# When a strip's norm is issued, and which engine adds its squares, in the fusions of the last two images

## The chip, the core and the metric

The kernel runs on one core of a Trainium2 chip. TensorE multiplies matrices, VectorE (DVE in the profile), ScalarE (ACT) and GpSimd (POOL) work elementwise, SyncE (SP) issues most transfers. The metric is the device time of one execution in microseconds (us); the median of several runs is compared.

## What is computed

The input is four images of 512 channels and 64 x 64 pixels, all in float32. Layer 0 is a linear attention with depthwise convolutions, a projection and the residual. Layer 1, cut to what matters here (`x` is layer 0's result):

```
E = stack([sobel, lap, diag, grad])                    # edge maps of x
ef = gelu(batch norm of (w_branch @ E))                # 4 branches, 512 channels
att = sigmoid(w_att2 @ gelu(w_att1 @ mean(ef) + b1) + b2)
z = w_fuse @ (ef * att) + b_fuse
zn = (z - mean_c(z)) / sqrt(var_c(z) + 1e-6)           # over the 512 channels
out = gelu(zn * ln_gamma + ln_beta) + x
```

The last three lines are the fusion. The kernel takes the mean out by centring the weights and the bias, so that the variance of a pixel is the sum of the squares of its 512 values of `z`, divided by 512.

## The kernel before

Four stages follow each other for an image: its attention (TensorE's convolutions and projections), `project_out` (products `yps`, writing layer 0's result `y` to memory), `edge_branches` (VectorE and ScalarE make `maps` from a window of `y`, TensorE multiplies them by the branch weights, products `br`, ScalarE's Gelu writes `ef` to memory), and `fuse_out`. Each stage is a Python generator that yields after a piece of work; the main loop runs one image's attention and lets the image before it advance behind it, by costs written out (`SHARE_F`, `FILL_F` and others, in estimated us). TensorE's order is exactly the order in which the program issues its products. On the other engines and on SP the framework orders the instructions by its own estimate, within what the data allow; each engine then works through its queue strictly in order.

At the end no attention is left. The last image's `project_out` and `edge_branches` (in taller steps of 8 rows, `side == "left"`) are interleaved with the third image's fusion through `fill` (L1001): after each edge step, as many yields of the fusion are taken as `FILL_F` and `FILL_EACH` say. Then the last image's fusion runs alone. I number images 0 to 3.

The fusion of an image (L794) goes over 8 strips of 512 pixels (`pieces`; the last strip of image 3 is cut into two halves of 256). For a strip it loads four chunks `ef`, and for each of four chunks `c` of output channels calls `fuse(c)` (L845):

- L848: four products into a PSUM bank `zps`, with the weights `wf_sb`
- L850: ScalarE squares it, with the bias, into `total` (c = 0) or `sq`
- L853 or L855: the value itself is drained, with the bias, to a buffer `z`, by ScalarE for image 2 and by VectorE for the others; there are 6 such buffers
- L858: for c > 0 GpSimd adds `sq` to `total`

`norm` (L860) finishes a strip: L864 multiplies `total` by a matrix of ones, so that each partition holds the sum over all channels (product `var`, in a PSUM bank); L866 is ScalarE's square root, L867 VectorE's reciprocal. Then for each chunk: SP loads `yr`, a part of `y` (L872, two buffers), VectorE multiplies `z` by the reciprocal (L875), ScalarE applies the Gelu (L876), GpSimd adds `yr` (L879), and SP stores `z` to `out` (L880). Only when that store has landed is the buffer of `z` free. The norm of a strip is held back and issued within the next strip's four calls: after the second of them (L900). `zps`, `var` and the small products of the attention weights share four PSUM banks in rotation (`ps_tile`); the tall edge step uses four others.

So TensorE's order in a strip is `zps` 0, `zps` 1, `var` of the strip before, `zps` 2, `zps` 3. A product can start only when the bank that was used four products of this kind earlier has been read.

Of the kernel before, what the change touches and what calls it, by code (L numbers as in the profile page):

```python
# [8 lines left out]
F32 = mybir.dt.float32  # L9
# [4 lines left out]
B, C, H, W = 4, 512, 64, 64  # L14
N = H * W
P = 128
NCH = C // P
# [72 lines left out]
def conv_seq_kernel(  # L90
    ctx: ExitStack, tc, x, wqkv, dpk, wtab, proj, projc, pwk, bn0, consts, vec, watt1, batt1, watt2, wbr, wfuse, out
):
    nc = tc.nc
# [18 lines left out]
    def ps_tile(name):  # L112
        return psum.tile([P, 512], F32, tag="ps", name=name)
# [8 lines left out]
    def rows(ap, width=W):  # L122
        return ap.rearrange("p (r c) -> p r c", c=width)
# [79 lines left out]
    def center_bias():  # L203

        fb_ps = ps_tile("fb_ps")
        nc.tensor.matmul(fb_ps[:, 0:4], lhsT=ones, rhs=vec_sb[:, V_FB, :], start=True, stop=True)
        fb_mean = const.tile([P, 1], F32, name="fb_mean")
        nc.vector.tensor_reduce(fb_mean, fb_ps[:, 0:4], AX.X, ALU.add)
        nc.vector.tensor_scalar(fb_mean, fb_mean, 1.0 / C, None, ALU.mult)
        nc.vector.tensor_scalar(fbias, vec_sb[:, V_FB, :], fb_mean, None, ALU.subtract)  # L210
# [583 lines left out]
    def fuse_out(b, efs, pool_sb, side):  # L794

        y = ys[b % 2]
        with ExitStack() as stack:
            pool = stack.enter_context(tc.tile_pool(name=f"F{b}", bufs=2, side=side, reuse_waits="tile"))
            wf_sb = pool.tile([P, NCH, C], F32, name="wf_sb", bufs=1)
            nc.sync.dma_start(out=wf_sb, in_=wfuse)  # L800
            watt1_sb = pool.tile([P, NCH, 64], F32, name="watt1_sb", tag="sq", bufs=3)
            nc.sync.dma_start(out=watt1_sb, in_=watt1)
            watt2_sb = pool.tile([64, C], F32, name="watt2_sb", tag="sq", bufs=3)
            nc.sync.dma_start(out=watt2_sb, in_=watt2)
            wf_mean = small.tile([P, NCH], F32, name="wf_mean")
            nc.vector.tensor_reduce(wf_mean, wf_sb, AX.X, ALU.add)
            nc.vector.tensor_scalar(wf_mean, wf_mean, 1.0 / C, None, ALU.mult)
            yield 0.0


            pooled = small.tile([P, 4], F32, name="pooled")
            nc.vector.tensor_reduce(pooled, pool_sb, AX.X, ALU.add)
            yield 14.0
            if b == 0:
                center_bias()
            hid_ps = ps_tile("hid_ps")
            for k in range(4):
                nc.tensor.matmul(
                    hid_ps[0:64, 0:1], lhsT=watt1_sb[:, k, :], rhs=pooled[:, k : k + 1], start=(k == 0), stop=(k == 3)
                )  # L820
            hid = small.tile([64, 1], F32, name="hid")
            nc.scalar.activation(hid, hid_ps[0:64, 0:1], AF.Gelu, bias=batt1_sb, scale=1.0 / N)
            yield 4.0
            att_ps = ps_tile("att_ps")
            for k in range(4):
                nc.tensor.matmul(att_ps[:, k : k + 1], lhsT=watt2_sb[:, ts(k, P)], rhs=hid, start=True, stop=True)
            att = small.tile([P, 4], F32, name="att")
            nc.vector.tensor_add(att, att_ps[:, 0:4], vec_sb[:, V_ATT2, :])
            nc.scalar.activation(att, att, AF.Sigmoid)

            for k in range(4):
                nc.vector.tensor_scalar(
                    wf_sb[:, k, :], wf_sb[:, k, :], wf_mean[:, k : k + 1], att[:, k : k + 1], ALU.subtract, ALU.mult
                )
            yield 8.0


            share = SHARE_F / (NJ * 5)


            pieces = [(j, 0, 512) for j in range(NJ)]
            if b == B - 1:
                pieces[-1:] = [(NJ - 1, 0, 256), (NJ - 1, 256, 512)]

            def fuse(c, ef, zs, total, n):  # L845
                ps = ps_tile("zps")[:, :n]
                for k in range(4):
                    nc.tensor.matmul(ps, lhsT=wf_sb[:, k, ts(c, P)], rhs=ef[k], start=(k == 0), stop=(k == 3))  # L848
                sq = total if c == 0 else pool.tile([P, 512], F32, name="sq", tag="sq", bufs=3)[:, :n]
                nc.scalar.activation(sq, ps, AF.Square, bias=fbias[:, c : c + 1])  # L850
                z = pool.tile([P, 512], F32, name="z", tag="z", bufs=6)[:, :n]
                if b == B - 2:
                    nc.scalar.activation(z, ps, AF.Identity, bias=fbias[:, c : c + 1])  # L853
                else:
                    nc.vector.tensor_scalar(z, ps, fbias[:, c : c + 1], None, ALU.add)  # L855
                zs.append(z)
                if c:
                    nc.gpsimd.tensor_add(total, total, sq)  # L858

            def norm(piece, zs, total):  # L860
                j, first, end = piece
                n, high = end - first, (end - first) // W
                ps = ps_tile("var")[:, :n]
                nc.tensor.matmul(ps, lhsT=ones, rhs=total, start=True, stop=True)  # L864
                rstd = pool.tile([P, 512], F32, name="rstd", tag="rstd", bufs=1)[:, :n]
                nc.scalar.activation(rstd, ps, AF.Sqrt, bias=ln_eps, scale=1.0 / C)  # L866
                nc.vector.reciprocal(rstd, rstd)  # L867
                at = 8 * j + first // W + 1
                for c in range(NCH):
                    z = zs[c]  # L870
                    yr = pool.tile([P, 8 * WB], F32, name="yr", tag="yr")[:, : high * WB]
                    nc.sync.dma_start(  # L872
                        out=yr, in_=y[c].rearrange("p r w -> p (r w)")[:, at * WB : (at + high) * WB]
                    )
                    nc.vector.tensor_mul(z, z, rstd)  # L875
                    nc.scalar.activation(  # L876
                        z, z, AF.Gelu, bias=vec_sb[:, V_LNB, c : c + 1], scale=vec_sb[:, V_LNG, c : c + 1]
                    )
                    nc.gpsimd.tensor_add(rows(z), rows(z), rows(yr, WB)[:, :, 1 : W + 1])  # L879
                    nc.sync.dma_start(out=out[b, c, :, 512 * j + first : 512 * j + end], in_=z)  # L880

            held = None
            for piece in pieces + [None]:
                if piece:
                    j, first, end = piece
                    n = end - first
                    ef = []
                    for k in range(4):
                        t = pool.tile([P, 512], F32, name="ef", tag="ef", bufs=8)[:, :n]
                        nc.sync.dma_start(out=t, in_=efs[j][:, k, first:end])  # L890
                        ef.append(t)
                    zs = []
                    total = pool.tile([P, 512], F32, name="total", tag="total")[:, :n]
                    fuse(0, ef, zs, total, n)
                    yield share
                    fuse(1, ef, zs, total, n)
                    yield share
                else:
                    yield 6.0
                if held:  # L900
                    norm(*held)
                    yield share
                if piece:
                    fuse(2, ef, zs, total, n)
                    yield share
                    fuse(3, ef, zs, total, n)
                    yield share
                    held = piece, zs, total

    def stages(b, heads, cheads, folded, side="right"):  # L910

        efs = [dram.tile([P, 4, 512], F32, name=f"ef{j}") for j in range(NJ)]
        pool_sb = small.tile([P, 4, 2 * NJ if side == "right" else NJ], F32, name="pool_sb")
        return [
            project_out(b, heads, cheads, folded, side), edge_branches(b, efs, pool_sb, side),
            fuse_out(b, efs, pool_sb, side),
        ]
# [201 lines left out]
```

## Time and profile before

| what | us |
|---|---|
| median of 3 runs | 5017.47 |
| lowest and highest of them | 5010.55, 5027.52 |
| the profiled execution's own time | 5033.35 |
| its span, first to last instruction | 5031.6 |
| TensorE busy in it | 4694.3 |
| VectorE, ScalarE, GpSimd busy in it | 2083.3, 1581.8, 397.3 |
| first `zps` of image 2's last stretch | 4651.0 |
| last `br` ends | 4857.5 |
| first `zps` of image 3 | 4871.8 |
| last `var` starts | 5013.2 |

The mean granted clock of TensorE was 0.971 of full speed. A line of the timeline gives start, duration, engine, line and operation, output and inputs, shapes and count; a bracket at its end gives how long the engine had been idle before it and what ended that. A line of the waits gives the waiting and the awaited instruction, then the total in us, the number of waits and the longest. The page's row of digits is the busy share of 40 equal slices of the span, in tenths.

### The profile page before, as it was taken

The page shows a single profiled execution, that of the slowest core. Times are in us where ns is not written, and L with a number is a line of the kernel's source. Part 1 is how long each engine was busy: PE and PEld are TensorE (multiplying, and loading weights), DVE is VectorE, ACT ScalarE, POOL GpSimd, SP SyncE. Part 2 cuts the span into 40 slices and gives each one's busy share as a digit, 9 for nine tenths or more (in the row PEclk, how much of TensorE's full clock was granted, in tenths as well). Part 3 has the DMA queues.
Part 4 walks back from the last instruction along what each step waited for, and adds up shares of the span by engine and source line. Part 5 has one row for each costly group of instructions (what it writes and reads, how often), then busy time and mean ns, then how long its engine had stood idle before and what let it go on. Part 6 is the DMA issues. An engine that isn't in the chain of part 4 may idle for free. (4 is left out here: it accounts for less than half of the span.)

```text
span 5031.6 us, 106279 instructions
## 1 busy us (share of the span) xinstructions
PE 4694.3 (93%) x46140; PEld 2689.2 (53%) x46140; DVE 2083.3 (41%) x2761; ACT 1581.8 (31%) x2712; POOL 397.3 (8%) x298
## 2 busy tenths in 40 slices
PE   9999999999999999799899999989999899899887
PEld 5655654455666554354465656445446565444333
DVE  1222222115565533311355553441125555447955
ACT  2112111003454423200245442430014445214765
POOL 0000000000000012100000000220000000000445
PEclk9999999999999999899999999999999999899998
DMA  6434467775666566677565566647665555575435
GB/s 198 138 119 134 134 192 194 162 163 161 193 190 189 180 187 189 192 177 167 152 189 189 186 192 183 207 153 217 149 173 176 171 173 170 162 166 144 165 125 163
DMA packets 627940, 864.04 MB, mean 172 GB/s; under 512 B 324073, under 2 KB 381449, under 8 KB 609041
## 3 DMA queue, kind: packets, MB, share of 16 engines
q1 hardware_dynamic: 548880, 756.51, 52.4%
q10 hardware_dynamic: 78592, 100.74, 6.3%
q8 instruction: 362, 5.93, 0.5%
q14 instruction: 106, 0.86, 0.1%
HBM read 575.93 MB, written 213.98 MB: 157 GB/s over the span
## 5 line engine op out<-in xcount | busy, mean ns | idle before, releaser
L268 PE MATMUL proj<-xt,w_sb 128*128 128x512 f32 x2048 | 955.9, 610 | 56.7 <-DMA xt<-in_x 34.6
L661 PE MATMUL yps<-hd,fold_sb 128*128 128x512 f32 x2048 | 907.8, 599 | 18.5 <-DMA hd<-heads 16.2
L402 PE MATMUL cv<-inp,mat 32*32 32x512 f32 x20480 | 728.3, 593 | 36.0 <-issue 28.2
L268 PEld LDWEIGHTS proj<-xt,w_sb 128*128 128x128 f32 x2048 | 382.7, 194 | 528.0 <-issue 451.6
L661 PEld LDWEIGHTS yps<-hd,fold_sb 128*128 128x128 f32 x2048 | 386.1, 191 | 511.0 <-issue 458.8
L402 PEld LDWEIGHTS cv<-inp,mat 32*32 32x32 f32 x20480 | 419.8, 103 | 313.1 <-issue 151.9
L848 PE MATMUL zps<-ef,wf_sb 128*128 128x512 f32 (+1 forms) x1056 | 473.4, 601 | 36.4 <-DMA ef<-ef 19.4
L290 PEld LDWEIGHTS val<-w_sb,xt 128*128 128x128 f32 x4096 | 470.6, 192 | 33.2 <-issue 25.9
L290 PE MATMUL val<-w_sb,xt 128*128 128x128 f32 x4096 | 485.2, 277 | 0.1
L738 PE MATMUL br<-maps,wbr_sb 128*128 128x256 f32 (+1 forms) x1792 | 474.2, 418 | 3.7 <-DVE s_sb L335 2.9
L274 ACT COPY strip<-proj 128x512 f32<-128x512 f32 x256 | 149.3, 583 | 932.5 <-PE proj L268 912.0
L666 DVE SCALAR_TENSOR_TENSOR yt<-yps,shift,xr 128x512 f32<-128x512 f32 x128 | 96.0, 750 | 836.5 <-PE yps L661 780.0
L738 PEld LDWEIGHTS br<-maps,wbr_sb 128*128 128x128 f32 x1792 | 340.9, 193 | 146.9 <-issue 102.0
L457 PE MATMUL corr<-near,ckt 128*32 128x160 f32 x8192 | 333.7, 315 | 40.3 <-DMA near<-near 32.9
L848 PEld LDWEIGHTS zps<-ef,wf_sb 128*128 128x128 f32 x1056 | 205.3, 198 | 285.5 <-issue 235.9
L247 POOL TENSOR_TENSOR mat<-dp_sb 128x1280 f32<-128x1280 f32 x32 | 76.7, 2398 | 3484.8 <-PE cv L402 2882.9
L457 PEld LDWEIGHTS corr<-near,ckt 128*32 128x32 f32 x8192 | 257.2, 111 | 136.1 <-issue 78.6
L714 DVE TENSOR_TENSOR maps<-dv 128x1054 f32<-128x1054 f32 (+1 forms) x112 | 158.0, 1411 | 376.3 <-PE br L738 376.2
L318 ACT ACTIVATE kt<-tr 128x512 f32<-128x512 f32 x128 | 75.9, 593 | 529.8 <-PE tr L316 401.2
L366 DVE RECIPROCAL rec<-rec 128x512 f32<-128x512 f32 x64 | 214.4, 3351 | 1.7
L746 ACT ACTIVATE ef_o<-br,shift,scale 128x256 f32<-128x256 f32 (+1 forms) x224 | 131.4, 590 | 228.1 <-PE br L738 210.4
L415 ACT ACTIVATE co<-cv 128x256 f32<-128x256 f32 x256 | 94.0, 398 | 331.1 <-PE cv L402 310.6
(127 smaller groups left out, 4049.2 us busy)
## 6 DMA issues: line engine op xcount, KB each, us to landing
xt<-in_x SPq DMA_DIRECT2D x316, 512.0 KB
near<-near SPq DMA_DIRECT2D x512, 264.0 KB
inp<-strip ACTq DMA_DIRECT2D x1024, 64.0 KB
win<-y SPq DMA_DIRECT2D x96, 396.0 KB
near<-vt SPq DMA_DIRECT2D x512, 66.0 KB
y<-yt SPq DMA_DIRECT2D x128, 264.0 KB
heads<-q SPq DMA_DIRECT2D x128, 256.0 KB
cheads<-cq SPq DMA_DIRECT2D x128, 256.0 KB
```

Source lines behind the costliest of these rows:

```text
L268: nc.tensor.matmul(ps, lhsT=self.w[t][:, c, :], rhs=xs[self.b, j][c], start=(c == 0), stop=(c == NCH - 1))
L274: nc.scalar.copy(s, ps)
L290: nc.tensor.matmul(ps[:, ts(c, P)], lhsT=xs[self.b, j][n][:, ts(c, P)], rhs=self.w[VALUE][:, n, :], start=(n == 0), stop=(n == NCH - 1),)
L366: nc.vector.reciprocal(rec, rec)
L402: nc.tensor.matmul(rows(banks[i])[32 * j : 32 * j + 32, :, c0:c1], lhsT=self.mat[t][q, j, (dx + 2) * 8 + 4 * b : (dx + 2) * 8 + 4 * b + 4, :],
L457: nc.tensor.matmul(self.banks[jj][32 * i : 32 * i + 32, 160 * b : 160 * b + 160], lhsT=self.held["c", i][:, at : at + 32], rhs=v[:, 4 * n ...
L661: nc.tensor.matmul(ps, lhsT=fold_sb[g // NG][:, g % NG, ts(c, P)], rhs=hd[g], start=(g == 0), stop=(g == 2 * NG - 1),)
L666: nc.vector.scalar_tensor_tensor(yt[:, :, 1 : W + 1], rows(ps), shift0[:, c : c + 1], rows(xr), ALU.add, ALU.add)
L714: nc.vector.tensor_sub(flat[:, half : 3 * half - 2], dvs[:, 2 : 2 * half], dvs[:, 0 : 2 * half - 2])
L738: nc.tensor.matmul(rows(ps), lhsT=wbr_sb[:, k, c, :], rhs=rows(maps[:, slot[k], c % 2, :], WB)[:, :, 0:W], start=(c == 0), stop=(c == NCH ...
L746: nc.scalar.activation(o[:, n, :], parts[n], AF.Gelu, bias=shift1[:, k : k + 1], scale=scale1[:, k : k + 1], accum_out=pool_sb[:, k, u : u ...
L848: nc.tensor.matmul(ps, lhsT=wf_sb[:, k, ts(c, P)], rhs=ef[k], start=(k == 0), stop=(k == 3))
```

## The change

Three things, in the fusions of images 2 and 3 (`late`) or of image 3 alone:

- the norm of the strip before is issued after the third call of `fuse`, no longer after the second;
- there are 8 buffers of `z` in place of 6;
- in image 3 alone, VectorE instead of GpSimd adds `sq` to `total`.

```diff
+            late = b >= B - 2
+
...
-                z = pool.tile([P, 512], F32, name="z", tag="z", bufs=6)[:, :n]
+                z = pool.tile([P, 512], F32, name="z", tag="z", bufs=8 if late else 6)[:, :n]
...
-                    nc.gpsimd.tensor_add(total, total, sq)
+                    (nc.vector if b == B - 1 else nc.gpsimd).tensor_add(total, total, sq)
...
+                if piece and late:
+                    fuse(2, ef, zs, total, n)
+                    yield share
                 if held:
                     norm(*held)
                     yield share
                 if piece:
-                    fuse(2, ef, zs, total, n)
-                    yield share
-                    fuse(3, ef, zs, total, n)
-                    yield share
+                    for c in range(3 if late else 2, NCH):
+                        fuse(c, ef, zs, total, n)
+                        yield share
                     held = piece, zs, total
```

A strip still yields five times, so the interleaving with the edge steps keeps its grid: `var` and the third `zps` change places. The framework orders the queues of VectorE, ScalarE, GpSimd and SP anew for the changed program.

## The prediction

> **What bounds the kernel now.** I read the page first, then TensorE's timeline and waits from 4640 us on, then the other engines there.
>
> ```profile
> span 5031.6 us, 106279 instructions
> PE 4694.3 (93%) x46140; PEld 2689.2 (53%) x46140; DVE 2083.3 (41%) x2761; ACT 1581.8 (31%) x2712; POOL 397.3 (8%) x298
> DVE  1222222115565533311355553441125555447955
> POOL 0000000000000012100000000220000000000445
> ```
>
> TensorE fills nine tenths of the span, so only its idle time can be won. The edited code runs in the last two images' fusions, in the last three slices of 126 us: GpSimd at 4, 4, 5, VectorE at 9, 5, 5.
>
> Two stages lie there. Stage A (4651 to 4857.5) holds image 2's fusion with image 3's edge products `br` between; stage B (4871.8 to the end) is image 3's fusion alone. The window view gives them; after the stretch come its length and the busy time of PE, PEld, DVE, ACT, POOL, then PEclk:
>
> ```profile
> 4651.00:4857.50 206.50, 183.21 (x398) 78.60 (x397) 171.88 (x114) 145.72 (x174) 85.91 (x46) 0.93 0.46 150
> 4871.80:5013.90 142.10, 126.52 (x306) 60.45 (x306) 83.57 (x82) 76.03 (x98) 75.46 (x61) 0.95 0.55 171
> ```
>
> In A VectorE is the nearest rival to TensorE; in B nothing but TensorE is near full. The idle gaps are in TensorE's timeline, the bracket naming what ended each:
>
> ```profile
> 4707.45 2.05 PE L864 MATMUL var<-total,ones 128*128 128x512 f32 x2 [7.37 <-ACT z L853]
> 4709.29 8.67 PE L738 MATMUL br<-maps,wbr_sb 128*128 128x512 f32 x16
> 4717.80 13.89 PE L848 MATMUL zps<-ef,wf_sb 128*128 128x512 f32 x32
> ...
> 4825.84 2.07 PE L864 MATMUL var<-total,ones 128*128 128x512 f32 x2 [5.40 <-POOL total L858]
> 4827.71 9.19 PE L738 MATMUL br<-maps,wbr_sb 128*128 128x512 f32 x16
> ...
> 4941.33 1.12 PE L864 MATMUL var<-total,ones 128*128 128x512 f32 x2 [1.37 <-DVE z L855]
> 4958.17 1.12 PE L864 MATMUL var<-total,ones 128*128 128x512 f32 x2 [1.06 <-DVE z L855]
> ```
>
> TensorE stops at the norm's product `var` because a PSUM bank is still held by an undrained `z`. The waits from 4640 on say why:
>
> ```profile
> DVE z L855 <- DMA out<-z: 44.2, 24, 4.4
> POOL z L879 <- DMA yr<-y: 34.3, 13, 4.5
> ACT z L853 <- DMA out<-z: 19.1, 15, 4.0
> ```
>
> With six `z` buffers the third product of a strip needs the buffer whose store the norm just issued has yet to finish. So the norm's latency (reciprocal, multiplies, Gelu, GpSimd's add of `yr`, store) is a loop that closes once per strip.
>
> **What the skill says.** "TensorE: Matmul & The Clock Gate", Part 1: after an idle window of about 3.4 us the array runs at half clock until it has been busy as long. The trace agrees: `var` takes 2.05 after 7.37 us of idling against 1.02 otherwise, and the 16 `br` behind it 8.67 against 7.03. "SBUF — State Buffer", section "SBUF: two separate sides": a VectorE operation with two SBUF inputs and a GpSimd one reading SBUF lock each other out. It agrees: beside GpSimd an edge operation takes 2.2 instead of 1.25 us, a GpSimd add up to 4.3 (12.78 for three) instead of 1.27. "GPSIMD Engine Reference", 4.1: elementwise adds are about twice as slow there. Four multiplies of this shape take 2.48 us on VectorE undisturbed (0.62 each), the add on GpSimd 1.27: agrees.
>
> **The parts.**
>
> (1) *Eight buffers and the norm one product later, priced together.* I count the distance from a norm's `var` to the latest moment at which a store must have freed its `z`. A product takes 3.43 us (13.74 from start to start for 4), `var` 0.86. Before, the first stored `z` frees the third product, whose bank the next `var` needs: 0.86 + 4 x 3.43 = 14.6 us later. After, it frees the next strip's first product, whose bank that strip's last product needs: 2 x 0.86 + 4 x 3.43 = 15.4. That is only 0.86 more; the second store has 18.9 instead of 15.4, the third 22.3 instead of 18.9, the fourth 29.2 instead of 22.3. The later pairs, late because they wait for `yr` (two buffers, reloaded only after GpSimd's adds), stop being critical; the first does not.
>
> Stage B. A norm's stores landed 6.7, 8.1, at most 13.0 and 15.5 us after its first multiply (4967.08; `z` released at 4973.81, 4975.23, 4980.09, 4982.55). I walked strips through the built queues, each step starting when its engine, its inputs and its buffer are there, with the trace's durations (square or Gelu 0.7, table load 1.28, reciprocal 3.35, GpSimd add 1.2, store 2.2, `yr` load 3). The two queues alternate in form. In one form the Gelus stand before the next strip's first square: from `var` at 0 the root ends at 2.8, the multiplies run at 7 to 10, the Gelus at 9 to 12, stores land at 13.3, 14.5, 19.2, 20.4. The next norm's reciprocal then stands behind the third `z` of its strip, which needs the store of 19.2: multiplies 9.4 after that `var`. Its first `z` waits for an add, whose square stands behind the Gelus, until 15.8 and drains at 16.55; TensorE wants the bank at 15.45. So 1.1 us of waiting in two strips, (2 x 14.6 + 1.1) / 2 = 15.15 a strip. The trace has 15.35, 16.64, 16.84, 16.44 and 16.15. From the first to the sixth norm (4894.74 to 4974.61) are 79.87 us; after it is 5 x 14.6 and some 2.5 of waits, 75.5. But the first norm is one product later, 3.43: net 0.9 earlier. From the sixth norm to the end the trace has 57.0; the walk gives 50.8, since the gap of 4.13 at 4990.76 and its cold products (2.8) fall away, and the last two half strips hold one product less. Stage B: **7 us**.
>
> Stage A. Gaps before `br` ends: 7.37 + 3.91 + 0.38 + 1.20 + 4.71 + 0.31 + 5.40 = 23.3; cold products: four `var` at 1.03 extra, two `br` groups (1.64, 2.16) and two pairs (2.18, 1.78), 12.0. Together 35.3. The last map is there at 4830.3 and its `br` starts at 4850.5; VectorE idled 10.4 us since 4670 (1.35, 1.16, 7.91), so the maps allow at most 4820, 31 earlier. I walked this stage also (us after 4600, VectorE's operations at 1.17, doubled beside GpSimd). TensorE runs without a gap to 111, where the second norm's `var` finds the `total` just added. ScalarE's root of it stands behind the third step's maps and ends at 127; on VectorE its reciprocal, which stands a whole edge step later than before, runs at 132 and the multiplies at 136 to 139, the Gelus at 138.5 to 141. The fourth strip's first `z` stands on ScalarE behind the next maps' square root, which waits for VectorE until 143, and drains at 147. TensorE, at 133 done with the third norm's `var`, wants that bank for the strip's last product: it stands for 14 us and pays 3 cold. From there the walk has `br` groups at 174, 192, 214 and 232, with waits under 2 us (the trace before: 176.9, 203.1, 227.7, 250.5). So the last is 18 us earlier, as 35.3 - 17 says: **18 us**. The attention weights' chain (4857.3 to 4871.8, 14.4 us) loses a wait: its sigmoid no longer stands behind four Gelus; the walk gives 13.2: **1 us**.
>
> Every instruction of the norm moves: two transfers for each of four chunks on SP. Their order among themselves stays; the next strip's `ef` loads stand behind them but are issued a strip ahead (4948.39 for products after 4974), hence nothing; without that lead it would be 3.4 us a strip. GpSimd's adds of the norm move past the `total` adds, counted in the walk.
>
> (2) *VectorE adds the squares in the last image.* Off GpSimd: 27 adds, 21 at 1.27 and 6 at 0.73, 31 us of its 75. On VectorE: no row shows this add. Its nearest is the multiply, 0.62 undisturbed; the upper bound is GpSimd's 1.27; I take 0.7, 2.1 us a strip on an engine with 9.3 of 14.6 filled (four `z` at 0.75, 3.35, multiplies of 2.5 to 3.5). At 1.27 it is 13.1, still under TensorE; below 0.62 at most 0.3 a strip are won. The add waits for ScalarE's square, and behind it stand the next `z` and the reciprocal, for which TensorE waits; this is the 1.1 us in two strips above. Without the move, GpSimd's adds would stand between the norm's own.
>
> (3) *Memory.* Two more buffers cost no time; the load of image 2's weights gets one more wait, on ScalarE (4366.28, needed at 4648); at worst a Gelu, under 1 us.
>
> **Sum.** 18 + 1 + 7 = 26. The profiled execution took 5033.35 (span 5031.6 and 1.75 around it): 5007.4. It stands 15.9 above the median of 5017.47; on the median 26 less is 4991.5.
>
> **Rivals.**
> - *The stall only moves* (R1): the reciprocal's later place on VectorE eats stage A. For: VectorE is at 172 of 206 us there. Against: it has 10.4 us of idling. One more stand of 14 + 3 us leaves 26 - 17 = 9: 5008.5.
> - *Down to VectorE's limit* (R2): no stand in the fourth strip. For: map 5 is ready 22 us sooner in the new order. Against: `z` drains in order. 31 + 1 + 10 = 42: 4975.5.
> - *Slower* (R3): the same stand, reciprocal late on VectorE and `z` behind the square root on ScalarE, in every second strip of image 2. Four stands are 4 x 17 = 68 against 35.3 lost now, less 8 from the rest: 25 slower, 5042. It decides from the third stand, since (35.3 + 8) / 17 = 2.5. For: in the new order the fourth, sixth and eighth strips have the pattern. Against: from the fifth strip on the walk has the store land before `z`'s turn.
>
> **How the numbers follow.** Forecast 0.62, R1 0.20, R2 0.08, R3 0.10. A measurement tells 0.3% (15 us) from no change. Forecast: walk errors of 12 us either way, 4980 to 5003, nearly all faster (0.60). R2 faster; R1 mostly within (0.18); of R3 a fifth within. Faster 0.60 + 0.08 + 0.01 of R1 = 0.69; same 0.02 + 0.18 + 0.02 = 0.22; slower 0.01 + 0.08 = 0.09. The range reaches from near R2 over R1 to 5016, leaving out R3 and the far part of R2: 4978 to 5016.
>
> **What would show it.** Right: waits of `z` for `out` in stage B fall from 44 us to under 25; strips there take 14.6 to 15.5; GpSimd's busy time falls to about 365; in stage A one gap over 10 us, before the fourth strip's last product, and the last `br` about 18 us earlier. Wrong: several gaps over 6 us in stage A, ended by ScalarE's `z`; or in B gaps of over 2 us ended by VectorE's `z` behind an add. If `br` waits for maps, R2 holds.

## The result, and the profile after

The changed kernel is faster, but by half of what was forecast. Over 16 runs of each its median is 5004.99 us against 5017.89 for the kernel before: a ratio of 0.9976, with a 95% interval of 0.9965 to 0.9987, or 12.9 us less (6.5 to 17.6). Forecast were 26 us. The profiled execution took 5007.84 us, with a span of 5006.1.

First the lines of the page of the changed kernel that answer to those of before:

```profile
span 5006.1 us, 106244 instructions
PE 4682.3 (94%) x46140; PEld 2687.1 (54%) x46140; DVE 2099.5 (42%) x2788; ACT 1580.6 (32%) x2713; POOL 369.7 (7%) x271
DVE  1222222114565624311356553441125565537966
POOL 0000000000000012200000000220000000000343
```

GpSimd has lost 27.6 us, and in the last slices VectorE has them: the move of the adds is there. Now the two stages, by the same window view (stretch, its length, busy time of PE, PEld, DVE, ACT, POOL with counts, PEclk, DMA share, GB/s). From here on stage A runs from the first `zps` of image 2 to the end of the last `br`, and stage B from the first `zps` of image 3 to the end of the span, in every kernel alike. The changed kernel:

```profile
4643.41:4836.11 192.70, 174.24 (x398) 76.23 (x397) 170.52 (x114) 144.11 (x173) 88.49 (x46) 0.96 0.47 152
4849.60:5006.10 156.50, 125.49 (x306) 60.58 (x306) 101.99 (x116) 83.54 (x109) 51.44 (x44) 0.89 0.55 170
```

Before they took 206.5 and 159.8 (4871.8 to 5031.6), with 14.3 for the chain of the attention weights between, now 13.5. So the stages gain 13.8 + 0.8 + 3.3 = 17.9 us; of the 25.5 by which the spans differ, the other 7.6 lie upstream, in code that the change doesn't touch. (The lines of the code stand two lower after the change: `zps` is L850, `z` L855 and L857, `total` L860, `var` L866.)

TensorE's timeline of the changed kernel in stage A, every line with a gap over 1 us and one neighbour:

```profile
4740.11 8.78 PE L850 MATMUL zps<-ef,wf_sb 128*128 128x512 f32 x16 [14.99 <-ACT z L855]
4748.73 7.03 PE L738 MATMUL br<-maps,wbr_sb 128*128 128x512 f32 x16
...
4794.05 15.70 PE L850 MATMUL zps<-ef,wf_sb 128*128 128x512 f32 x32 [2.24 <-ACT z L855]
...
4817.84 1.12 PE L866 MATMUL var<-total,ones 128*128 128x512 f32 x2 [1.23 <-POOL total L860]
```

The one long stand is where it was forecast, before the fourth strip's last product. It costs 14.99 and 1.75 of slow products behind it (8.78 for 16 instead of 7.03). ScalarE shows what the awaited `z` stood behind:

```profile
4736.14 1.28 ACT L734 ACT_TABLE_LOAD   x1 [3.77 <-DVE maps L733]
4737.43 2.05 ACT L734 ACTIVATE maps<-maps,sobel_eps 128x2104 f32<-128x2104 f32 x1
4739.39 1.25 ACT L855 ACTIVATE z<-zps,fbias 128x512 f32<-128x512 f32 x2
```

It is the square root of the next maps, which waits for VectorE; the `z` drains right behind it. Counted from the start of the stage that is at 92.7 and 96.0 us, where the forecast had 92 and 96. Two smaller gaps follow, of 2.24 and 1.23 us. In stage B:

```profile
4934.12 1.12 PE L866 MATMUL var<-total,ones 128*128 128x512 f32 x2
4938.05 15.66 PE L850 MATMUL zps<-ef,wf_sb 128*128 128x512 f32 x32 [2.80 <-DVE z L857]
...
4964.55 1.12 PE L866 MATMUL var<-total,ones 128*128 128x512 f32 x2 [1.37 <-DVE total L860]
4968.54 8.86 PE L850 MATMUL zps<-ef,wf_sb 128*128 128x256 f32 x32 [2.86 <-DVE z L857]
4977.93 0.70 PE L866 MATMUL var<-total,ones 128*128 128x256 f32 x2 [0.52 <-DVE total L860]
4981.57 3.02 PE L850 MATMUL zps<-ef,wf_sb 128*128 128x256 f32 x8 [2.95 <-DVE z L857]
4986.60 1.22 PE L866 MATMUL var<-total,ones 128*128 128x256 f32 x2 [2.00 <-DVE total L860]
```

The strips from 4875 on take 14.60, 14.59, 15.07, 14.61 and then 19.43 us from `var` to `var`. The gap of 2.80 has its reason on VectorE and ScalarE just before it:

```profile
4933.39 0.68 DVE L860 TENSOR_TENSOR total<-total,sq 128x512 f32<-128x512 f32 x1
4936.56 0.69 DVE L860 TENSOR_TENSOR total<-total,sq 128x512 f32<-128x512 f32 x1 [2.49 <-ACT sq L852]
4937.24 0.75 DVE L857 TENSOR_SCALAR z<-zps,fbias 128x512 f32<-128x512 f32 x1
```

```profile
4933.02 2.93 ACT L878 ACTIVATE z<-z,vec_sb 128x512 f32<-128x512 f32 x4
4935.86 1.24 ACT L852 ACTIVATE sq<-zps,fbias 128x512 f32<-128x512 f32 x2
```

Four Gelus hold back ScalarE's square until 4935.86; the add that VectorE now makes waits 2.49 us for it; behind the add stands the `z` whose bank TensorE wants. TensorE's next product starts at 4938.05.

### The profile page after: what moved, and what is told of

The parts are those of the page before. It is cut to its first block, busy times and chain, and to the rows that moved or that the text cites. A ratio compares the mean times of both kernels' runs of the same rounds, so it can differ in the third digit from the quotient of the medians.

```text
span 5006.1 us, 106244 instructions
## 1 busy us (share of the span) xinstructions
PE 4682.3 (94%) x46140; PEld 2687.1 (54%) x46140; DVE 2099.5 (42%) x2788; ACT 1580.6 (32%) x2713; POOL 369.7 (7%) x271
## 5 line engine op out<-in xcount | busy, mean ns | idle before, releaser
L850 PE MATMUL zps<-ef,wf_sb 128*128 128x512 f32 (+1 forms) x1056 | 468.8, 597 | 56.5 <-DMA ef<-ef 19.0
L850 PEld LDWEIGHTS zps<-ef,wf_sb 128*128 128x128 f32 x1056 | 203.4, 196 | 299.7 <-issue 229.1
L881 POOL TENSOR_TENSOR z<-z,yr 128x512 f32<-128x512 f32 (+1 forms) x132 | 175.9, 1351 | 293.5 <-ACT z L878 172.5
```

## The experiments

Two theories stood at the start. Mine: the forecast's mechanism holds, six buffers' loop is broken by buffers and late norm together, and only sizes are off. The rival: the gain is the buffers' alone, and the late norm and VectorE's adds give nothing or cost. The stages make a sharper measure than the whole time, because whole executions of one kernel scatter by 10 us and more (the kernel before: 5006.22 to 5028.59); so each kernel below is given by the lengths of stages A and B in its profile, and by a ratio to the kernel before where it was timed.

**The parts one by one.** Four kernels. `b8` is the changed kernel with the norm back after two products and GpSimd's adds, which leaves only the buffers; `b8dve` keeps VectorE's adds; `latepool` is the changed kernel without the move of the adds; `dve` is the kernel before with that move alone.

The norm back in its place, in `b8` and `b8dve`:

```diff
-                if piece and late:
+                if False:
-                    for c in range(3 if late else 2, NCH):
+                    for c in range(2, NCH):
```

GpSimd's adds, in `b8` and `latepool` (in `dve`, on the kernel before, the same line the other way round):

```diff
-                    (nc.vector if b == B - 1 else nc.gpsimd).tensor_add(total, total, sq)
+                    nc.gpsimd.tensor_add(total, total, sq)
```

> Eight buffers of z alone in the last two images; the norm again after two products, the squares again added by GpSimd. Stage A is 206.5 us before and 192.7 after the whole change, stage B 159.8 and 156.5, the chain between 14.3 and 13.5; together 380.6 and 362.7. My theory (buffers and order are worth something only together, since the var product waits for a total that GpSimd has just added): stage A about 200, stage B about 158.5, together some 372, so about 8 us faster than before. Rival (the buffers carry the whole gain, and the order nothing): stage A 193 or less, stage B 157 or less, together 363 or less, some 18 us faster.

> Eight buffers and VectorE's adds in the last image; the norm again after two products. Against the eight buffers alone, stage A cannot change. My theory: the adds take GpSimd's queue off the path to var, so stage B is 1 to 2 us shorter than with the buffers alone, about 157. Rival (the adds wait behind Gelus on VectorE and hold up z and the reciprocal): stage B is as long or up to 3 us longer than with the buffers alone.

> The changed kernel with GpSimd adding the squares in the last image too: eight buffers and the late norm remain. Stage A as after the change, 192.7 within 2. My theory (without the move GpSimd's adds of squares stand between the norm's own): stage B 158 to 160 instead of 156.5. Rival (the move gives back what it wins): stage B 156.5 or less, and no gaps that end on VectorE's total.

> The kernel before, with VectorE adding the squares in the last image and nothing else changed. Stage A as before, 206.5 within 2. My theory: the loop through six buffers binds, so stage B stays within 1.5 us of 159.8, and the whole within 0.1% of before. Rival (the adds alone shorten the norm's way over GpSimd, adds of yr and stores come earlier): stage B 156 to 158. Second rival (VectorE's adds are waits): stage B above 161.5.

Measured:

| kernel | buffers, norm, adds in image 3 | stage A | stage B | ratio to before |
|---|---|---|---|---|
| before | 6, early, GpSimd | 206.5 | 159.8 | |
| `dve` | 6, early, VectorE | 204.7 | 157.9 | 0.9994 [0.9985, 1.0003] |
| `b8` | 8, early, GpSimd | 207.9 | 146.0 | 0.9986 [0.9978, 0.9995] |
| `b8dve` | 8, early, VectorE | 207.4 | 147.0 | 0.9983 [0.9975, 0.9992] |
| `latepool` | 8, late, GpSimd | 192.3 | 151.2 | 0.9962 [0.9948, 0.9975] |
| after | 8, late, VectorE | 192.7 | 156.5 | 0.9976 [0.9965, 0.9987] |

Both theories fall, each in one stage. In stage B the buffers alone win 13.8 us (11.7 against a second profile of the kernel before, told below); the late norm then gives back 5.2, and VectorE's adds another 5.3 (only 1.0 with the early norm). In stage A it is the reverse: eight buffers with the early norm win nothing, and the late norm is worth 15. The move of the adds never paid in stage B: not in `b8dve`, where a gain of 1 to 2 us was expected, and not after the late norm, where its absence was expected to cost. With six buffers it changed nothing: the 157.9 of `dve` is the 157.7 of that second profile. The 5.3 us rest on the stages, one profile of `latepool` against two of the changed kernel; the timed ratios of the two overlap. TensorE's timeline of `b8` in stage B shows what the changed kernel could have had:

```profile
4934.02 1.02 PE L866 MATMUL var<-total,ones 128*128 128x512 f32 x2
4934.88 10.48 PE L850 MATMUL zps<-ef,wf_sb 128*128 128x512 f32 x32
4947.20 1.12 PE L866 MATMUL var<-total,ones 128*128 128x512 f32 x2 [1.84 <-POOL total L860]
4948.17 7.07 PE L850 MATMUL zps<-ef,wf_sb 128*128 128x256 f32 x32
```

No gap until the last whole strip's `var`, and five strips of 14.6 us each from one `var` to the next. In stage A of the same kernel:

```profile
4769.65 6.17 PE L850 MATMUL zps<-ef,wf_sb 128*128 128x512 f32 x14
4792.19 2.08 PE L866 MATMUL var<-total,ones 128*128 128x512 f32 x2 [16.37 <-POOL total L860]
4794.06 9.00 PE L738 MATMUL br<-maps,wbr_sb 128*128 128x512 f32 x16
```

With the norm only two products behind its strip, `var` stands 16.37 us for a `total` whose square is late on ScalarE: it runs at 4789.63, behind Gelus and maps, though its product had ended at about 4769. With the late norm one product more lies between, and in the four profiles with eight buffers and the same code in image 2 (`latepool`, `mix2`, the changed kernel twice) no `var` of the stage waits more than 2.85 us for its `total`.

**Is it the distance?** The prediction had counted how long after a norm's `var` a store must have freed its `z`: 14.6 us with six buffers and the early norm, 15.4 with eight and the late one. It never counted eight with the early norm: there the first stored `z` frees the next strip's first product, and the bank of that is wanted by the strip's last product, a product and a `var` later than with six buffers: 0.86 + 5 x 3.43 + 0.86 = 18.9. So the late norm takes back 3.4 of what the buffers give. Seven buffers test this by number: 15.4 with the early norm, 14.6 with the late one. `early7` and `late7` are `b8` and `latepool` with `bufs=7`.

> Seven buffers of z in both images, the norm after two products, GpSimd adds. My theory for stage B now (all that counts is the distance in products from a norm's var to the moment at which the first store must have freed its buffer: 14.6 us with six buffers early, 15.4 with eight late or seven early, 18.9 with eight early, 14.6 with seven late): stage B 151 (149 to 153), as with eight late and GpSimd's adds. Rival (the place of the norm by itself costs, through its engines' queues): stage B 146 to 148, as with eight early.

> Seven buffers of z in both images, the norm after three products, GpSimd adds. By the distance (14.6 us, as with six buffers early): stage B 157 to 160. Rival (the place of the norm by itself costs, the buffers beyond the first new one nothing): stage B 150 to 153, as with eight late.

Stage B came to 150.0 and 158.1: seven early is within 1.2 us of eight late (151.2), and seven late within 1.7 us of six early (157.7 and 159.8), whatever the place of the norm. So the length of the stage goes with the distance, and the rival's figures, 146 to 148 and 150 to 153, are both missed. (In stage A these two took 207.0 and 198.3: with seven buffers the late norm is worth 8.7.)

Where in the stage the time goes is another matter. The table cuts stage B at the first and the sixth `var`, by TensorE's timeline, in us; between them lie five whole strips, 73.0 without any wait.

| kernel | distance | to the first `var` | five strips | behind the sixth `var` |
|---|---|---|---|---|
| before, first and second profile | 14.6 | 22.98, 22.39 | 79.87, 78.36 | 56.99, 56.93 |
| `late7` | 14.6 | 25.71 | 76.72 | 55.68 |
| `early7` | 15.4 | 22.95 | 74.38 | 52.66 |
| `latepool` | 15.4 | 25.83 | 73.08 | 52.32 |
| `b8` | 18.9 | 22.67 | 72.95 | 50.38 |
| after, first and second profile | 15.4 | 25.65, 25.83 | 78.30, 78.33 | 52.55, 53.11 |

With the late norm one product more (3.43 us) stands ahead of the first `var` and one less behind the sixth. The whole strips follow the distance, but from 18.9 to 15.4 they lose only 0.1 to 1.4 us. What the late norm costs lies behind the sixth `var`: `latepool` has one product less to do there than `b8` and takes 1.9 us longer, 5.4 more of waits and slow products. Its two long gaps there are of 4.42 and 4.27 us; that of 4.27 stands at the first half strip, where `b8` has none:

```profile
4930.75 10.01 PE L850 MATMUL zps<-ef,wf_sb 128*128 128x256 f32 x32 [4.27 <-DVE z L857]
```

A half strip's products take half as long (7.07 us for 32, 13.90 in a whole strip), so the same number of products is a shorter time there. That fits the distance; no run tests it alone. The cost of VectorE's adds lies in the whole strips: 78.30 against 73.08.

**Together.** `mix2` takes from each stage what it wants: eight buffers in both, late norm in image 2 only, GpSimd's adds.

```diff
-                if piece and late:
+                if piece and b == B - 2:
-                    for c in range(3 if late else 2, NCH):
+                    for c in range(3 if b == B - 2 else 2, NCH):
```

> Eight buffers in both images, the norm late in image 2 only, GpSimd adds the squares in both. If what the parts did alone adds up (late norm wins in image 2 and costs in image 3, VectorE's adds cost): stage A 192.5 as after the change, the chain 13.5, stage B 146 as with the buffers alone; together 352, 28.6 us less than before, a ratio of about 0.9943. Rival (the stages are not independent: image 3's start hangs on how image 2 ends): stage B 149 or more.

Stage A 194.0, stage B 146.3, with the chain 353.8: as added up, within 2 us. The ratio is 0.9958 [0.9938, 0.9978], the forecast one was 0.9943.

**The stand of 15 us in stage A.** `z10` is `mix2` with ten `z` in image 2 paid for with two `ef`; `z9sq3` has nine, paid for with one of image 3's `sq`; `z10sq` ten, with two `sq` in both images; `zdve` keeps eight and drains the first `z` of each strip of image 2 on VectorE.

The buffers of `z10`:

```diff
-                z = pool.tile([P, 512], F32, name="z", tag="z", bufs=8 if late else 6)[:, :n]
+                z = pool.tile([P, 512], F32, name="z", tag="z", bufs={B - 2: 10, B - 1: 8}.get(b, 6))[:, :n]
-                        t = pool.tile([P, 512], F32, name="ef", tag="ef", bufs=8)[:, :n]
+                        t = pool.tile([P, 512], F32, name="ef", tag="ef", bufs=6 if b == B - 2 else 8)[:, :n]
```

`z10sq` has the same `z`, all eight `ef`, and in the three tiles with the tag `sq` `bufs=2 if b >= B - 2 else 3`; `z9sq3` has 9 for the 10 and `bufs=2 if b == B - 1 else 3`. In `zdve`:

```diff
-                if b == B - 2:
+                if b == B - 2 and c:
```

> The kernel of mix2 with ten z buffers in image 2, paid for by six instead of eight ef buffers there. My theory of the 15 us stand in stage A (the fourth strip's first z waits for the store of the second strip's first z, and by then stands behind the maps' square root): that store has been out for a whole strip, so the z drains at once and the stand falls to under 5 us; stage A 180 to 186. Rival (it is ScalarE's order behind the square root, whatever the buffers): the stand stays at 13 or more, stage A 190 or more. Stage B 146 in both.

> The kernel of mix2 with nine z buffers in image 2 and all eight ef buffers, the room taken from image 3's squares (sq two instead of three). My theory of the 15 us stand: it is the store of the second strip's first z that the fourth strip's first z waits for, and with nine buffers that z takes one freed a strip earlier; only the strip's second z still waits, whose bank is wanted at least one product and a br group later. The stand falls from 15 to under 6, stage A 180 to 187, so 7 to 14 below mix2. Rival (ScalarE's order behind the maps' square root): the stand stays at 13 or more and stage A at 192 to 194. Stage B 146 to 149 (two sq buffers may cost).

> Ten z buffers in image 2 with all eight ef buffers, two sq buffers in both images. My theory: the stand at the fourth strip's last product is gone and no wait for ef takes its place; stage A 178 to 185. Rival (TensorE's stand moves on to the maps or to the sq buffers): stage A 188 or more. Stage B 146 to 149.

> The kernel of mix2 with the first of each strip's four z in image 2 drained by VectorE instead of ScalarE (eight buffers). My theory: the z waits for the store all the same, so the stand before the fourth strip's last product shrinks only by what the maps' square root adds, from 15 to about 10, and the z may now stand on VectorE behind map operations: stage A 186 to 194. Rival (the square root ahead of it on ScalarE is the whole cause): the stand under 4, stage A 182 or less.

The stand went from 15.14 (`mix2`) to 6.13 with nine buffers and 4.29 with ten, so a freer buffer does take most of it away, as thought. How much of that is the store itself isn't separated: the buffers also changed ScalarE's order, in which the `z` now stands ahead of the maps' square root (4699.27 against 4704.38 in `z10sq`), where in `mix2` it stood behind it (4722.71 against 4720.75). And stage A did not get shorter: 196.4 and 195.4. The ratios are 0.9963 [0.9949, 0.9977] and 0.9958 [0.9944, 0.9972]. In `z10sq` the time comes back further on:

```profile
4699.99 5.40 PE L850 MATMUL zps<-ef,wf_sb 128*128 128x512 f32 x8 [4.29 <-ACT z L855]
...
4745.03 2.08 PE L866 MATMUL var<-total,ones 128*128 128x512 f32 x2 [3.57 <-POOL total L860]
...
4760.19 16.50 PE L850 MATMUL zps<-ef,wf_sb 128*128 128x512 f32 x32 [5.62 <-ACT z L855]
...
4785.61 1.99 PE L866 MATMUL var<-total,ones 128*128 128x512 f32 x2 [2.06 <-POOL total L860]
```

These four gaps come to 15.5 us, against 15.14, 1.13 and 2.85 in `mix2`, and each is followed by slow products. `zdve` says little: its stand stayed at 14.32 (stage A 196.4), but the `z` had then VectorE's map operations ahead of it. And `z10` ran into another wait: stage A 207.8 (ratio 0.9981 [0.9972, 0.9991]), with gaps of 5.42, 7.00 and 16.72 us ended by the load of `ef`. That is the price of the lead of those loads, which the prediction had named as cover.

**What else holds stage A, and how good the first profile was.** `noyr` and `noyr10` are `mix2` and `z10sq` without one statement in image 2; `before2` and `after2` are the two kernels unchanged.

```diff
-                    nc.gpsimd.tensor_add(rows(z), rows(z), rows(yr, WB)[:, :, 1 : W + 1])
+                    if b != B - 2:
+                        nc.gpsimd.tensor_add(rows(z), rows(z), rows(yr, WB)[:, :, 1 : W + 1])
```

> The kernel of mix2 (eight buffers, norm late in image 2 only), with GpSimd's adds of yr left out in image 2, whose output so lacks the residual. If VectorE, slowed beside GpSimd, limits stage A: VectorE's busy time there falls from 170 to about 150 and stage A to 180 or less. If the loop through z and its store limits it: the norm's way is 1.2 to 3 us shorter, the stand shrinks by that, stage A 188 to 192.

> The kernel of z10sq (ten z buffers in image 2), with GpSimd's adds of yr left out in image 2, whose output so lacks the residual. If VectorE limits stage A once the stand is gone: stage A falls from 195.4 to 180 or less, with VectorE's busy time. If something else holds it (ScalarE's order, the total on GpSimd): stage A 190 or more.

> The kernel before once more, unchanged. If its first profile had stages that were long by chance: stage A 204 to 205, stage B 157 to 158.5, together with the chain 376 to 377 instead of 380.6. If the loss lies upstream in the changed kernels: 380 to 381 again. The ratio tells what a comparison of the kernel with itself gives: 1.000 within 0.001.

> The changed kernel once more. Stage A 192 to 194, stage B 155.5 to 157.5, together 361 to 364; ratio 0.9965 to 0.9987. If its first profile was lucky: together 366 or more.

Without those adds stage A falls to 181.3 and 174.9 us, and VectorE's busy time there from 170.4 to 154.8 and from 172.9 to 152.0. In `noyr`, with eight buffers, the stand falls to 8.85 and no later gap over 1 us is left in the stage; in `noyr10` the stand is gone, TensorE is at full clock and works 170.7 of 174.9 us:

```profile
4634.89:4809.79 174.90, 170.66 (x398) 75.10 (x397) 152.01 (x114) 143.62 (x174) 52.54 (x22) 1.00 0.40 139
```

So these adds of GpSimd's cost stage A 13 us with eight buffers and 21 with ten, in the stand as well as behind it. The Trainium skill ("SBUF — State Buffer", section "SBUF: two separate sides") says that a VectorE operation with two SBUF inputs and a GpSimd operation that reads SBUF shut each other out; the 16 and 21 us of VectorE's time that went with some 37 us of GpSimd's agree. Whether the stage waits for that, or for the adds' own latency in the norm, these two runs don't separate.

The second profiles give the sum once more. Windows of `before2`, then of `after2`:

```profile
4617.61:4822.01 204.40, 182.34 (x398) 78.23 (x397) 171.21 (x114) 145.53 (x174) 87.89 (x46) 0.93 0.46 150
4836.30:4994.00 157.70, 126.52 (x306) 60.59 (x306) 89.37 (x89) 83.09 (x108) 80.56 (x69) 0.91 0.53 166
```

```profile
4618.71:4811.01 192.30, 174.45 (x398) 76.33 (x397) 170.14 (x114) 144.11 (x173) 89.33 (x46) 0.96 0.46 152
4824.50:4981.80 157.30, 125.51 (x306) 60.30 (x306) 100.69 (x116) 83.54 (x109) 51.85 (x44) 0.89 0.55 169
```

The kernel before took 376.4 us over its stages here, 380.6 in the first profile; the changed one 363.1, after 362.7. The stage A of `dve`, whose code there is that of the kernel before, was 204.7, so the first profile looks like the long one. The difference of the second pair, 13.3, is near what the timed runs say (12.9); the first pair's was 17.9. `after2` was timed at 0.9966 [0.9952, 0.9979], and the kernel before against itself at 0.9995 [0.9986, 1.0004].

**The squares on VectorE in image 2.** `dve2` is `z10sq` with the change's move of the adds applied to the other image.

```diff
-                    nc.gpsimd.tensor_add(total, total, sq)
+                    (nc.vector if b == B - 2 else nc.gpsimd).tensor_add(total, total, sq)
```

> The kernel of z10sq (ten z buffers and late norm in image 2, eight and early norm in image 3), with VectorE adding the squares up in image 2 and GpSimd in image 3. Of GpSimd's 89 us in stage A some 53 are adds of squares; leaving its adds of yr out (36 us) took 21 us from VectorE, so taking these out should take 53 x 21 / 36 = 31, against 24 adds of 0.68 us that come on: VectorE's busy time from 173 to about 158. If the engine's time limits stage A: 180 to 187. If the adds' place in VectorE's queue costs, as in image 3 with the late norm (they wait for squares behind Gelus and square roots, and maps stand behind them): stage A 195 or more. Stage B 146 in both.

Stage A fell to 181.6, stage B is 145.3, and the ratio is 0.9933 [0.9915, 0.9952], the lowest measured. Only the chain between them grew, from 13.5 to 17.1 us: TensorE waits 5.21 for VectorE's `wf_sb` there, 0.74 in `z10sq`. Stage A:

```profile
4638.27:4819.87 181.60, 173.52 (x398) 76.02 (x397) 173.13 (x136) 145.02 (x173) 39.14 (x22) 0.98 0.49 159
```

The length was as forecast, the reason was not: VectorE is busy 173.1 us, not 158. Its 22 adds within the stage cost 18.8, and its other operations win back as much, but no more. It is the idle time that went: VectorE's waits for ScalarE's root and maps fell from 7.5 + 6.3 to 0.5 + 2.4 us, while its adds wait 4.4 for squares, and TensorE's gaps over 1 us fell from 15.5 to 7.2. GpSimd's 49 us of adds had stood between the squares and `var`, and ahead of the norm's adds in GpSimd's queue; which of the two mattered more stays open.

## Why the prediction was right in sign and too large

The forecast of 26 us was 18 in stage A, 1 in the chain and 7 in stage B. Against the profile that it was made from, the change gave 13.8, 0.8 and 3.3; against the second pair 12.1, 0.8 and 0.4.

What failed are sizes. In stage A it is the step "with waits under 2 us" behind the stand, where 5.3 us were lost. In stage B it is part (2)'s wait of VectorE's adds, put at 1.1 us in two strips or 2.5 in five and measured at 5.3, together with the walk's end of that stage, put at 50.8 us and measured at 52.6. Some 5 us more are the first profile of the kernel before.

- *Part (1), stage A, 18 us: right in mechanism, 4 too large.* One stand of 14.99 + 1.75 = 16.7 us, in the place named, ended by the `z` named, which stood behind the square root named; forecast were 14 + 3. From the start of the stage the walk had the last four `br` groups at 123, 141, 163 and 181 us; they came at 123.3, 141.4, 166.2 and 185.7. What was missed are the two gaps ahead of the last two groups: 2.24 with 1.81 of slow products, and 1.23, together 5.3. At the first of them a `z` stands behind a maps' square root again, and the map operation awaited there took 2.24 us on VectorE. The prediction had taken slow products to follow idling of about 3.4 us; here they followed gaps of 2.24 and, in `latepool`, 2.08 us (15.70 for 32), though not one of 2.26 in `noyr10` (14.00). Stage A is 192.7 instead of 188.5. That removing the stand would bring nothing further was not seen.
- *Part (1), stage B: "priced together" is the step that hid the cost.* The distance was counted right and stage B goes with it: six early and seven late (14.6), seven early and eight late (15.4) and eight early (18.9) fall into three groups, 158 to 160, 150 to 151 and 146. But with the pair priced as one, the count for eight buffers and an early norm was never made. It is 18.9, and that kernel's stage B is 146.0, where the late norm, still with GpSimd's adds, has 151.2. That the forecast's 152.8 is near this 151.2 is chance, since it was made with VectorE's adds. The walk let the gap of 4.13 at the end fall away, but with 9.7 us the gaps behind the sixth `var` are nearly the 10.4 of before.
- *Part (2), VectorE's adds: the term that was mis-sized.* The add takes 0.68 us (forecast 0.7), GpSimd's page time fell to 369.7 (forecast about 365). But the wait for the square behind the Gelus, put at 1.1 us in two strips, costs 5.3 to 6.1 in all (156.5 and 157.3 against 151.2), nearly all of it in the whole strips and most in the fifth, at 19.43. The half strips' gaps are no part of it: `latepool` has as much there (9.9 us, the changed kernel 9.7). The prediction had given gaps of over 2 us ended by VectorE's `z` behind an add as the sign that it is wrong in stage B, and that sign is there. Its "without the move GpSimd's adds would stand between the norm's own" was argued, and the run without the move shows it worth less than nothing.
- *The chain of the attention weights:* 0.8 for 1, right. *Memory and the weights' load:* no wait for them turned up.
- *The `ef` loads' lead, costed at nothing:* right; without part of it stage A loses 12 to 14 us (`z10`, 207.8 against 195.4 in `z10sq` and 194.0 in `mix2`).
- *The sum's base:* the profiled execution of before was taken as it stood. Its stages were 4.2 us longer than in the second profile, 2.1 in each. That is nearly all that separates the 17.9 of the first pair of profiles from the 13.3 of the second; it is no error of a mechanism, but one execution's length.
- *Signs named ahead:* VectorE's waits of `z` for the store in stage B fell from 44.2 to 19.4 us (forecast under 25); one gap above 10 us in stage A; the last `br` 13.8 earlier instead of 18; four of the five whole strips at 14.6 to 15.1 us (forecast 14.6 to 15.5), the fifth at 19.43.
- *Rivals:* R1 (a second stand) gave 9 us, nearer the measured 12.9 than the forecast, but there was no second stand: small gaps and stage B made up for it. R2 had no stand in the fourth strip and VectorE as the next limit; with the stand cut to 4.29 (`z10sq`) stage A was no shorter, and it took GpSimd's adds away to shorten it. R3's stands did not come; nothing shows a second of that size.

So what is missing is 4 to 6 us in stage A and 4 to 7 in stage B; the larger figures, from the second pair, hold the 2.1 us by which each stage of the first base was too long.

## What to carry to other kernels

When a change alters both the number of buffers and the place of the step that frees them, count the distance from the freeing step to its first user for every combination, not only for the one proposed: here eight buffers with the old place had the longest distance in one stage, and the late place paid only in the other. Before work is moved to a faster engine, look at what stands behind it in that engine's queue and what it waits for: the same add cost 5.3 us where VectorE also drained the banks and the norm came late, at most 1.0 where it came early, and was the change behind a gain of 13.8 in stage A where ScalarE drained them. And profile the base twice when the forecast is of the size of its scatter: here its stages came out 4.2 us apart.

## What was not expected of the hardware

The stages of an execution repeat better than its whole time. Stage A, in four profiles with the same code in image 2, took 192.3 to 194.0 us, and stage B, in nine profiles with eight buffers, the early norm and GpSimd's adds in image 3, 145.3 to 147.0 (the kernel before gave 204.4 and 206.5, 157.7 and 159.8), while the point at which stage A begins lay anywhere from 4606.6 to 4651.0 us. A wait of 15 us cut to 4 brought nothing (stage A 194.0, then 195.4), since four smaller ones, each followed by slow products, took the place of the one. And a short gap can cost as much again in slow products: 2.24 us were followed by 1.81.
